# First layer of six experts by fifteen block products, with more buffers and later loads

## The chip, the core and the metric

The kernel runs on one NeuronCore of a Trainium2 chip. Its engines are TensorE (PE; its weight loads are listed apart, as PEld), VectorE (DVE), ScalarE (ACT), GpSimd (POOL) and SyncE (SP), each with a queue of its own that it works off in order, and 16 DMA engines that all queues share. The metric is the device time of one execution in microseconds, as the median of several runs; lower is better. All data is float32 unless marked.

## What is computed

1250 nodes with 768 features and 40,000 directed edges (and self-loops) go through a transformer-like block. Cut to what matters here:

```python
xn = layernorm(x)
x = x + gnn(xn, edges) + linear_attention(xn)        # two graph-attention layers; 12 heads
x = x + ffn(layernorm(x))

def ffn(xt):                                          # 1250 x 768, 8 experts, hidden 384
    gate = xt @ Wg + bg                               # 1250 x 8
    scores, idx = top_k(gate, 2)
    h = gelu(einsum('td,edh->eth', xt, W1) + b1)      # first layer, W1[e] is 768 x 384
    y = einsum('eth,ehd->etd', h, W2) + b2            # second layer, W2[e] is 384 x 768
    comb = sum(one_hot(idx, 8) * scores)              # the two raw gate scores of a token
    return einsum('te,etd->td', comb, y)
```

The change concerns the first layer of the experts, which the kernel computes only for the tokens that chose the expert.

## The kernel before, in words

Up to about 865 us the kernel builds the graph's adjacency matrix, runs the two attention layers (lines 380 to 640), the linear attention (640 to 1040) and the router. The last stage of that, by pairs of 125-token tiles, writes the normalised tokens with their eight gate values to `xl_d` in DRAM (`finish`, L929; stores at L937 and L951) and the sum so far to `out`, and counts each token into a table of slots: `idx` gives, for every expert and every block of 128 places, the rows of `xl_d` that stand there. Already there, products of big matrices are done by seven products of quarters with sums beside them (`query`, and `P` in the loop over pairs).

The experts then run in a Python loop, unrolled, of eight slots. Every expert has `FIX` = 3 fixed blocks of 128 rows; what is over goes into extra blocks, of which the first is placed into the slots of experts 6 and 7 (`more_...`) and others into a loop at the end. One slot, for e = 0 to 6, consists of

- `inner` (L1081): the first layer. The result `hT` is hidden-major: three tiles of 128 hidden units by 384 tokens. For each hidden tile six matmuls (128 of the 768 features each) accumulate in a PSUM bank, W1's 128x128 block as the stationary operand and `xT` with 384 token columns as the moving one; ScalarE then applies Gelu with the bias from PSUM into SBUF (L1092). Expert 0 does its first block alone, and then the other two, since their rows come later.
- `gather` (L1060) of the next expert: three indirect DMAs on POOL's queue (L1065) fetch 128 rows each into `xg` (three buffers); TensorE transposes them into PSUM tiles `px` (L1074, six transposes of 128 a block, two banks), VectorE copies them to `xsT` (L1075), and a tiny copy takes the expert's gate column into `gates` (L1078).
- `give` (L1095) three times, once per block: ScalarE multiplies the output bias with the gate (`gb`, L1099), TensorE multiplies `hT`'s block with W2 in two halves of 384 columns (`py`, L1106, four banks), VectorE combines them as `ys = py * gate + gb` (L1108, two buffers of `ys`), and an indirect DMA on POOL's queue adds the 128 rows to `out` in DRAM (L1110). These scatter-adds touch the same tensor, so each waits until the one before has landed.
- two loads on SP's queue: the output bias of expert e+2 (L1175) and the weights of expert e+4 (`expert`, L745; W1 at L748, W2 at L750, 1152 KB each) into one of four weight buffers `w`, when that buffer's last reader is done.

The weights of experts 1 to 3 are requested behind the router's last instructions, as soon as their buffers come free. The framework draws up the order of each engine's queue from the program's order and from when it expects operands and buffers to be free, and sets all waits; the queues of a trace are therefore not quite in the program's order.

A float32 matmul is seen in the trace as two passes: an `x36` of the first layer is 18 matmuls.

## Time and profile before

| what | value |
|---|---|
| median of 3 runs | 1096.91 us (1096.15 to 1099.57) |
| the profiled execution | 1097.82 us, its span 1096.1 us, mean granted clock 0.986 |
| start of the expert stage (first row gather issued) | 865.48 us |
| first row gather landed, first transpose | 871.95 us |
| first layer of expert 1, 2, 3 begins on TensorE | 901.11, 926.34, 951.56 us |
| last matmul ends | 1085.87 us |
| TensorE, weight loads, VectorE, ScalarE, POOL busy | 1031.0, 701.6, 705.8, 359.9, 78.8 us |
| one pass of the first layer, 384 columns, by its own row | 486 ns (passes overlap) |
| L1108, L1075 on VectorE, one | 616, 552 ns |
| scatter-add from issue to landing, min / median / max | 5.4 / 5.7 / 9.0 us |
| row gather from issue to landing, min / median / max | 3.7 / 5.4 / 6.4 us |

How to read the profile: a group's row gives line, engine, operation, out<-in with shapes, count, then busy time, mean duration of one, and the idle time of the engine just before them with what ended it. Durations of matmuls overlap each other, so the rate of a stream is read from its start and end, or from the chain. The chain is the sequence of work that ended last, followed back from the end of the run; each line gives start, length and what it was. A line can be written "PE ph L1090 x36": engine, tile written, line, instructions. The last part of the run, from 865 us on, is the expert stage and all that this document is about.

### The profile page before, as it was taken

To read this page: it belongs to the slowest core of one execution; us is meant where nothing else is said; L and a number is where in the kernel's file an instruction comes from. 1 tells how busy PE (TensorE), PEld (TensorE's weight loads), DVE (VectorE), ACT (ScalarE), POOL (GpSimd) and SP (SyncE) were. 2 spreads that over 40 slices of the span, in tenths; PEclk is the share of its full clock that TensorE was granted. 3 is DMA by queue.
4 is the path that set the end of the run, shared out by engine and by line. 5 is a ranking of instruction groups with operands and counts; after the bars stand their busy time and mean duration, and the time that the engine had idled before them with its cause. 6 is when DMAs were issued, how large, how long until landed. Compare 5 with 4: busy or idle time off the path is not lost.

```text
span 1096.1 us, 12392 instructions
## 1 busy us (share of the span) xinstructions
PE 1031.0 (94%) x4630; PEld 701.6 (64%) x4630; DVE 705.8 (64%) x1460; ACT 359.9 (33%) x548; POOL 78.8 (7%) x106
## 2 busy tenths in 40 slices
PE   6999999999999999988999999999999499999996
PEld 5876666587878879544555555656665376666674
DVE  7866684697897957769687958686855522222321
ACT  4612226372728373283833121112110111111121
POOL 2000000000000000000001000000000122223321
PEclk9999999999999999999999999999999699999998
DMA  5060000000000002000035002021144847777534
GB/s 161 29 211 19 29 15 1 1 1 1 1 1 1 1 1 87 1 0 1 15 142 153 1 15 71 20 65 43 58 153 132 274 116 221 213 213 203 116 58 59
DMA packets 35412, 79.51 MB, mean 73 GB/s; under 512 B 7078, under 2 KB 15416, under 8 KB 35348
## 3 DMA queue, kind: packets, MB, share of 16 engines
q1 hardware_dynamic: 29588, 58.90, 16.8%
q0 software_dynamic: 5760, 19.78, 8.5%
q8 instruction: 37, 0.61, 0.2%
q14 instruction: 27, 0.22, 0.1%
HBM read 60.33 MB, written 18.34 MB: 72 GB/s over the span
## 4 chain that ended last, share of the span: by engine, by line
PE 73%; DVE 20%; DMA 2%; ACT 1%; issue 1%; POOL 0%; DVEq 0%; POOLq 0%; ACTq 0%
PE s L863 19%; PE mm L648 9%; PE ph L1090 9%; PE py L1106 8%; PE mm L477 8%; DVE scr L569 6%; DVE w L589 5%; DVE w L590 5%; PE ag L602 3%; PE mm L924 2%; PE ag L624 2%; PE ec L398 2%; PE mm L452 2%; PE px L1074 2%; PE rb L558 1%; PE mm L662 1%
## 5 line engine op out<-in xcount | busy, mean ns | idle before, releaser
L602 PE MATMUL ag<-kept,w 125*125 125x198 f32 x800 | 137.5, 333 | 5.1 <-DVE w L590 4.8
L602 PEld LDWEIGHTS ag<-kept,w 125*125 125x125 f32 x800 | 133.5, 188 | 9.0 <-DVE w L590 9.0
L1106 PE MATMUL py<-w,hT 128*128 128x384 f32 x300 | 100.9, 486 | 0.0
L1090 PE MATMUL ph<-xsT,w 128*128 128x384 f32 (+2 forms) x432 | 99.9, 390 | 0.0
L589 DVE TENSOR_TENSOR w<-v,w 125x1250 f32<-125x1250 f32 x60 | 86.3, 1453 | 6.0 <-ACT w L587 5.4
L648 PE MATMUL mm<-Wv_sb,xnT 128*125 128x384 f32 x240 | 85.6, 489 | 4.8 <-DVE kvacc L668 4.8
L1090 PEld LDWEIGHTS ph<-xsT,w 128*128 128x128 f32 x432 | 68.9, 191 | 30.3
L569 DVE CUSTOM_DVE_ANT_0 scr<-ss_row,mask 125x1250 bf16<-125x1250 f32 x60 | 87.2, 1453 | 1.6 <-ACT ss_row L560 1.2
L477 PE MATMUL mm<-Wg,xnT 128*125 128x400 f32 x240 | 87.7, 505 | 0.2 <-ACT xnT L367 0.2
L590 DVE SCALAR_TENSOR_TENSOR w<-w,AT 125x1250 f32<-125x1250 f32 x60 | 86.4, 1454 | 0.4
L588 ACT ACTIVATE v<-dn_row,sl 125x1250 f32<-125x1250 f32 x60 | 79.3, 1333 | 17.4 <-DVE w L589 16.9
L648 PE MATMUL mm<-Wk_sb,xnT 128*125 128x384 f32 x240 | 85.0, 487 | 0.0
L1108 DVE SCALAR_TENSOR_TENSOR ys<-py,gates,gb 128x384 f32<-128x384 f32 x50 | 30.3, 616 | 79.3 <-PE py L1106 54.7
L1106 PEld LDWEIGHTS py<-w,hT 128*128 128x128 f32 x300 | 55.1, 190 | 33.1
L1075 DVE COPY xsT<-px 128x384 f32<-128x384 f32 x50 | 25.8, 552 | 73.3 <-PE px L1074 73.3
L648 PEld LDWEIGHTS mm<-Wv_sb,xnT 128*125 128x125 f32 x240 | 42.5, 187 | 31.4 <-DVE kvacc L668 6.9
L477 PEld LDWEIGHTS mm<-Wg,xnT 128*125 128x125 f32 x240 | 42.5, 188 | 26.5 <-ACT xnT L367 0.9
L1099 ACT ACTIVATE gb<-spare,gates 128x768 f32<-128x768 f32 x24 | 22.4, 935 | 112.4 <-DVE ys L1108 94.8
L587 ACT ACTIVATE w<-up_row,s 125x1250 f32<-125x1250 f32 x40 | 53.2, 1331 | 17.7 <-PE ag L602 17.6
L648 PEld LDWEIGHTS mm<-Wk_sb,xnT 128*125 128x125 f32 x240 | 42.0, 187 | 22.7 <-issue 1.8
L863 PE MATMUL s<-w,xnT 128*125 128x384 f32 x150 | 55.4, 489 | 0.0
L863 PE MATMUL s<-w 128*125 128x384 f32 x150 | 53.9, 491 | 0.0
(328 smaller groups left out, 1515.1 us busy)
## 6 DMA issues: line engine op xcount, KB each, us to landing
w<-in_L_ffn_W_dram SPq DMA_DIRECT2D x18, 1152.0 KB
xt<-in_x_dram SPq DMA_DIRECT2D x20, 336.0 KB
out_dram<-xt SPq DMA_DIRECT2D x10, 336.0 KB
xl_d<-xl SPq DMA_DIRECT2D x10, 336.0 KB
spare<-in_L_ffn_b_dram SPq DMA_DIRECT2D x8, 384.0 KB
W_sb<-in_L_gnn_W_dram SPq DMA_DIRECT2D x1, 2304.0 KB
Wk_sb<-in_L_mix_Wk_dram SPq DMA_DIRECT2D x1, 2304.0 KB
Wv_sb<-in_L_mix_Wv_dram SPq DMA_DIRECT2D x1, 2304.0 KB
```

The source lines that it names most:

```text
L477: nc.tensor.matmul(ps[:PT, :2 * (CG + 2)], xnT[:, c, t * PT:(t + 1) * PT], Wg1[:, c, 2 * k:2 * k + 2].rearrange("p h c -> p (h c)"), start ...
L569: nc.vector.tensor_tensor_reduce(scr, ss_row, mask[:, t], 1.0, 0.0, ALU.mult, ALU.max, top[:, t:t + 1])
L587: nc.scalar.activation(w, up_row, AF.Exp, bias=ss[:, st:st + 1])
L588: nc.scalar.activation(v, dn_row, AF.Exp, bias=sl[:, st:st + 1])
L589: nc.vector.tensor_tensor(w, v, w, op=ALU.max)
L590: nc.vector.scalar_tensor_tensor(w, w, 2.0, AT[:, st, :N], op0=ALU.min, op1=ALU.mult)
L602: nc.tensor.matmul(ag[:, t // 2, o:o + CG], w[:, t * PT:(t + 1) * PT], gw[:, st, hd], start=st == 0 and t % 2 == 0, stop=st == NT - 1, ski ...
L648: nc.tensor.matmul(ps[:PT, :384], xnT[:, c, t * PT:(t + 1) * PT], w[:, c, half], start=c == 0, stop=c == KC - 1)
L863: nc.tensor.matmul(ps, left[:, c], right[:, c], start=start and c == 0, stop=c == n - 1, skip_group_check=True)
L1090: nc.tensor.matmul(ph[:, n], w[0][:, o:o + 128], xT[:, c, n], start=c == 0, stop=c == KC - 1)
L1106: nc.tensor.matmul(py[:, :384], hT[:, f, j * 128:(j + 1) * 128], w[:, o:o + 384], start=f == 0, stop=f == FC - 1)
L1108: nc.vector.scalar_tensor_tensor(ys[:, half], py[:, :384], gates, gb[:, half], op0=ALU.mult, op1=ALU.add)
```

## The change

The first layer of experts 1 to 6 is no longer 54 products of 128x128 blocks, run as 18 matmuls of 384 columns, but 45, run as 45 matmuls of 128 columns. W1 of an expert is seen as 3 (hidden) by 2 (halves of the features) blocks, the tokens as 2 by 3, each block being three tiles of 128x128 deep. Fifteen products of sums of such blocks replace the eighteen of the plain scheme: `WAYS[0]` gives the eleven sums or differences of weight blocks, `WAYS[1]` the eleven of token blocks, `PRODUCTS` the fifteen products, each with the bank that it opens or is accumulated onto, and the result blocks to which its bank is copied (by ScalarE) or added (by VectorE). The nine result blocks are gathered in `hT` in SBUF; the Gelu is then applied there, in place.

The weight sums of expert e+1 are handed to VectorE one by one between the products of expert e, and the token sums of expert e+1 stand behind its gather. The sums lie in memory that earlier stages left free (`xnT` and `kept`). For expert 1 both kinds stand in expert 0's slot, the weight sums between its `give`s. Expert 0, expert 7 and the extra blocks keep `inner`.

With it come other edits: all PSUM tiles of the stage come from one pool of eight banks; `xg` gets five buffers in place of three, `ys` three in place of two; the copies from `px` to `xsT` move from VectorE to ScalarE, except for expert 0; and the weights of experts 1, 2 and 3 are now loaded behind a tiny VectorE copy that writes a gate value of expert 1's first, second and third block into the weight buffer, so that each load starts only once these rows are there.

```diff
--- before.py
+++ after.py
@@ -64,6 +64,32 @@
     for s in ap.shape:
         n *= s
     return bass.AP(tensor=ap.tensor, offset=ap.offset, ap=[[0, parts], [1, n]])
+
+
+WAYS = ((("12", 5, 1, 6), ("13", 3, 1, 4), ("9", 1, -1, "13"), ("14", 3, -1, 1), ("15", 2, -1, "12"),
+         ("7", 1, 1, "15"), ("3", 2, -1, 6), ("8", 4, 1, 5), ("-2", 2, 1, "9"), ("1", 5, -1, 3),
+         ("5", 6, -1, 4)),
+        (("4", 5, -1, 2), ("2", 4, 1, 6), ("9", "2", -1, 3), ("14", 1, -1, "9"), ("7", 1, 1, 2),
+         ("11", 6, -1, 3), ("15", "7", -1, 5), ("3", "15", -1, 4), ("8", 3, -1, 5), ("1", 3, -1, 2),
+         ("5", 6, -1, 5)))
+
+
+PRODUCTS = (
+    ("6", None, 1, 1, (1, "="), (2, "=-")),
+    ("10", None, 2, 4, (1, "+"), (3, "=-"), (7, "=")),
+    ("12", None, "12", 5, (8, "="), (9, "=")),
+    ("4", None, 5, "4", (8, "-"), (5, "=-")),
+    ("9", None, "9", "9", (4, "=-"), (3, "-")),
+    ("14", "6", "14", "14", (4, "+")),
+    ("13", None, "13", 3, (3, "+"), (6, "=")),
+    ("7", "12", "7", "7", (2, "+")),
+    ("11", None, 4, "11", (4, "-"), (6, "+"), (9, "+")),
+    ("3", "4", "3", "3", (7, "+")),
+    ("8", None, "8", "8", (5, "-")),
+    ("2", None, "-2", "2", (3, "+")),
+    ("15", None, "15", "15", (2, "-"), (7, "-")),
+    ("1", "13", "1", "1", (5, "+")),
+    ("5", "8", "5", "5", (9, "+")))
 
 
 @with_exitstack
@@ -742,9 +768,13 @@
 
     fp = ctx.enter_context(tc.tile_pool(name="fp", bufs=1, side="right"))
 
-    def expert(w1, w2, b2, b):
+    def expert(w1, w2, b2, b, behind=None):
+
 
         t = wt.tile([128, KC, D], F32, name="w", bufs=4).rearrange("p c f -> p (c f)")
+        if behind is not None:
+            nc.vector.tensor_copy(t.rearrange("p (a f) -> p a f", a=2)[:1, :, 0],
+                                  behind.to_broadcast([1, 2]))
         nc.sync.dma_start(t[:, :KC * FF].rearrange("p (c f) -> p c f", c=KC),
                           w1.rearrange("(c p) f -> p c f", p=128))
         nc.sync.dma_start(t[:, KC * FF:].rearrange("p (c d) -> p c d", c=FC),
@@ -1047,33 +1077,87 @@
         free = rp.tile([128, NV], F32)
         nc.vector.tensor_scalar(free, inv, 0.0, nobody, op0=ALU.is_equal, op1=ALU.mult)
         nc.vector.scalar_tensor_tensor(idx[:, :NV], inv, -1.0, free, op0=ALU.add, op1=ALU.add)
-        for e in range(1, 4):
-            ring.append(expert(fW1[e], fW2[e], fb2[e] if e < 2 else None, spare[e % 2]))
 
 
     mix.close()
     sp = ctx.enter_context(tc.tile_pool(name="sp", bufs=2))
-    x_p = ctx.enter_context(tc.tile_pool(name="x_p", bufs=2, space=PSUM))
-    h_p = ctx.enter_context(tc.tile_pool(name="h_p", bufs=2, space=PSUM))
-    y_p = ctx.enter_context(tc.tile_pool(name="y_p", bufs=4, space=PSUM))
-
-    def gather(rows, e):
+    e_p = ctx.enter_context(tc.tile_pool(name="e_p", bufs=8, space=PSUM))
+    q3 = KC // 2
+    places = [xnT.rearrange("p c n -> p (c n)"), kept]
+    slot3 = lambda k: places[k % 2][:, k // 2 * q3 * 128:(k // 2 + 1) * q3 * 128].rearrange(
+        "p (c n) -> p c n", c=q3)
+
+    def bank():
+        return e_p.tile([128, 512], F32, name="ps")
+
+    def sums(blocks, side, at):
+
+        got = {k + 1: b for k, b in enumerate(blocks)}
+        todo = []
+        for k, (name, a, sign, b) in enumerate(WAYS[side]):
+            got[name] = slot3(at + k)
+
+            def make(name=name, a=a, sign=sign, b=b):
+                op = nc.vector.tensor_add if sign > 0 else nc.vector.tensor_sub
+                op(got[name], got[a], got[b])
+            todo.append(make)
+        return got, todo
+
+    def weight_sums(w, e):
+        v = w[0][:, :KC * FF].rearrange("p (g c f) -> p g c f", g=2, c=q3)
+        return sums([v[:, g, :, i * 128:(i + 1) * 128] for i in range(3) for g in range(2)], 0,
+                    e % 2 * len(WAYS[0]))
+
+    def token_sums(xT):
+        return sums([xT[:, g * q3:(g + 1) * q3, j * 128:(j + 1) * 128] for g in range(2)
+                     for j in range(3)], 1, 2 * len(WAYS[0]))
+
+    def inner15(A, B, bias, between):
+
+
+        hT = sp.tile([128, FC, FIX * 128], F32, name="hT")
+        C = [hT[:, i, j * 128:(j + 1) * 128] for i in range(3) for j in range(3)]
+        banks = {}
+        for name, onto, a, b, *uses in PRODUCTS:
+            ps = banks[name] = banks[onto] if onto else bank()
+            for c in range(q3):
+                nc.tensor.matmul(ps[:, :128], A[a][:, c], B[b][:, c], start=c == 0 and not onto,
+                                 stop=c == q3 - 1, skip_group_check=True)
+            for to, how in uses:
+                to = C[to - 1]
+                if how == "=":
+                    nc.scalar.copy(to, ps[:, :128])
+                elif how == "=-":
+                    nc.scalar.mul(to, ps[:, :128], -1.0)
+                elif how == "+":
+                    nc.vector.tensor_add(to, to, ps[:, :128])
+                else:
+                    nc.vector.tensor_sub(to, to, ps[:, :128])
+            if between:
+                between.pop(0)()
+        while between:
+            between.pop(0)()
+        for f in range(FC):
+            nc.scalar.activation(hT[:, f], hT[:, f], AF.Gelu, bias=bias[:, f])
+        return hT
+
+    def gather(rows, e, copy=nc.vector.tensor_copy):
 
         got = []
         for r in rows:
-            xg = sp.tile([128, D + NE], F32, name="xg", bufs=3)
+            xg = sp.tile([128, D + NE], F32, name="xg", bufs=5)
             nc.gpsimd.indirect_dma_start(xg, None, xl_d, bass.IndirectOffsetOnAxis(r, 0))
             got.append(xg)
         xT = sp.tile([128, KC, FIX * 128], F32, name="xsT")
         gates = sp.tile([128, FIX], F32, name="gates")
         for j, xg in enumerate(got):
             for a in range(2):
-                px = x_p.tile([128, 512], F32, name="px")
+                px = bank()
                 for c in range(3):
                     o = (3 * a + c) * 128
                     nc.tensor.transpose(px[:, c * 128:(c + 1) * 128], xg[:, o:o + 128], ident)
-                nc.vector.tensor_copy(xT[:, 3 * a:3 * a + 3, j * 128:(j + 1) * 128],
-                                      px[:, :384].rearrange("p (b n) -> p b n", b=3))
+                copy(xT[:, 3 * a:3 * a + 3, j * 128:(j + 1) * 128],
+                     px[:, :384].rearrange("p (b n) -> p b n", b=3))
             at = slice(D + e, D + e + 1) if isinstance(e, int) else bass.ds(e + D, 1)
             nc.vector.tensor_copy(gates[:, j:j + 1], xg[:, at])
         return xT, gates
@@ -1084,7 +1168,7 @@
             hT = sp.tile([128, FC, FIX * 128], F32, name="hT")
         n = slice(a * 128, b * 128)
         for f in range(FC):
-            ph = h_p.tile([128, 512], F32, name="ph")
+            ph = bank()
             for c in range(KC):
                 o = c * FF + f * 128
                 nc.tensor.matmul(ph[:, n], w[0][:, o:o + 128], xT[:, c, n], start=c == 0,
@@ -1097,10 +1181,10 @@
         w, wb = w
         gb = sp.tile([128, D], F32, name="gb")
         nc.scalar.mul(gb, wb, gates)
-        ys = sp.tile([128, D], F32, name="ys")
+        ys = sp.tile([128, D], F32, name="ys", bufs=3)
         for k in range(2):
             half = slice(k * 384, (k + 1) * 384)
-            py = y_p.tile([128, 512], F32, name="py")
+            py = bank()
             for f in range(FC):
                 o = KC * FF + f * D + k * 384
                 nc.tensor.matmul(py[:, :384], hT[:, f, j * 128:(j + 1) * 128], w[:, o:o + 384],
@@ -1153,24 +1237,41 @@
         nc.vector.tensor_mul(pick, vals, mine)
         one = fp.tile([128, 1], F32, name="one", bufs=2)
         nc.vector.tensor_reduce(one, pick, AX.X, ALU.add)
-        pr = h_p.tile([128, 512], F32, name="ph")
+        pr = bank()
         nc.tensor.transpose(pr[:1, :128], one, ident)
         nc.vector.tensor_scalar(row, pr[:1, :128], add, None, op0=ALU.add)
 
     for e in range(NE - 1):
         xT, gates = ahead
         bias = fb1T[:, :, e:e + 1]
+        between = []
+        if 0 < e < NE - 2:
+            A, between = weight_sums(ring[e + 1], e + 1)
         if e:
-            hT = inner(ring[e], xT, bias)
+            hT = inner15(now, B, bias, between)
+            now = A
         else:
             hT = inner(ring[e], xT, bias, 0, 1)
             inner(ring[e], xT, bias, 1, FIX, hT)
-        ahead = gather(fixed(e + 1), e + 1)
+        ahead = gather(fixed(e + 1), e + 1, nc.scalar.copy)
+        if e == 0:
+            for n in range(1, 4):
+                ring.append(expert(fW1[n], fW2[n], fb2[n] if n < 2 else None, spare[n % 2],
+                                   ahead[1][:1, n - 1:n]))
+        todo = []
+        if e < NE - 2:
+            B, todo = token_sums(ahead[0])
+        if e == 0:
+            now, between = weight_sums(ring[1], 1)
+        for make in todo:
+            make()
         if e == NE - 2:
             ee, more_rows, more_bias, more_w = first
             more_xT, more_gates = gather([more_rows], ee)
         for j, rows in enumerate(fixed(e)):
             give(ring[e], hT, j, rows, gates[:, j:j + 1])
+            for make in between[j * 6:(j + 1) * 6]:
+                make()
         if e + 2 < NE:
             nc.sync.dma_start(spare[e % 2], row_bcast(fb2[e + 2], 128))
         if e + 4 < NE:
```

## The prediction

> **What bounds the kernel now.** I read the page first (busy shares, the chain), then the chain in order of time through the experts, then a table of stretches, then groups and queues of that part.
>
> ```profile
> PE 1031.0 (94%) x4630; PEld 701.6 (64%) x4630; DVE 705.8 (64%) x1460; ACT 359.9 (33%) x548; POOL 78.8 (7%) x106
> PE 73%; DVE 20%; DMA 2%; ACT 1%; issue 1%; POOL 0%; DVEq 0%; POOLq 0%; ACTq 0%
> ```
>
> TensorE is busy almost throughout. The chain from the router's end on:
>
> ```profile
> 865.48 6.42 DMA xg<-xl_d,idx
> ...
> 901.27 11.61 PE ph L1090 x36
> 916.18 10.32 PE py L1106 x32
> 926.50 11.61 PE ph L1090 x36
> 941.40 10.32 PE py L1106 x32
> ...
> 1039.94 3.71 DMA xg<-xl_d,rows
> ...
> 1054.31 8.04 PE ph L1090 x72
> ```
>
> Experts follow every 25.2 us (901.27, 926.50) and the chain never leaves TensorE. A logical f32 product is two passes: 36 passes of 384 columns take 11.61 us, 322.5 ns each, and the 72 passes of 128 columns late in the run take 8.04 us, 111.7 ns each. Two row gathers are on the chain as transfers: the first (6.42 us) and the one for the extra block (3.71 us).
>
> ```profile
> 864.00:868.00 4.00, 0.58 (x2) 0.11 (x2) 0.93 (x7) 0.00 (x0) 2.03 (x2) 0.50 1.04 406
> 868.00:872.00 4.00, 0.05 (x1) 0.06 (x1) 0.07 (x1) 0.00 (x0) 0.95 (x1) 0.50 0.90 353
> 926.30:951.60 25.30, 25.30 (x92) 15.50 (x91) 6.91 (x15) 4.54 (x6) 7.70 (x6) 1.00 0.76 203
> ```
>
> The columns are the stretch, its length, busy time of PE, PEld, DVE, ACT, POOL, then granted clock, DMA share and GB/s. During the first gather the DMA engines are full and TensorE is idle; in an expert's stretch TensorE has no gap, while VectorE works 6.91 of 25.30 us and ScalarE 4.54.
>
> ```profile
> 919.70 1.61 POOL L1110 DMA_INDIRECT out_dram<-ys,idx  x1 [2.13 <-DVE ys L1108]
> 927.68 1.59 POOL L1110 DMA_INDIRECT out_dram<-ys,idx  x1 [6.37 <-DVE ys L1108]
> 937.36 1.55 POOL L1110 DMA_INDIRECT out_dram<-ys,idx  x1 [8.09 <-DMA out_dram<-ys,idx]
> 944.92 1.61 POOL L1110 DMA_INDIRECT out_dram<-ys,idx  x1 [2.14 <-DVE ys L1108]
> ```
>
> The scatter-adds run one at a time: 7.98, 9.68 and 7.56 us from start to start, a second chain almost as long as an expert.
>
> **The change, part by part.**
>
> *The products.* For experts 1 to 6, 36 passes of 384 columns (11.61 us) become 15 products of 3 matmuls, 90 passes of 128 columns. At 111.7 ns that is 10.05 us: 1.56 us saved per expert, 9.4 us over six. The row is the same operand shape, each pass with its own weight load, so I take it. Neighbours bound it: the 36 passes from 1066.05 last 4.18 us with their tail, 116 ns (10.45 us, 7.0 saved); a third of the wide pass, 107.5 ns, would give 9.68 us (11.6 saved). Transposes (2.0 us) and the second layer (36 passes, 11.6 us) stay, so the expert's floor is 23.7 us.
>
> *What VectorE gets.* Per expert 22 sums of 384 elements and 16 additions of 128 from PSUM; it loses six copies (L1075, 552 ns).
>
> ```profile
> L1018 DVE TENSOR_TENSOR xt<-xt,s 125x384 f32<-125x384 f32 x25 | 13.7, 552 | 36.5 <-PE s L863 36.4
> L960 DVE TENSOR_TENSOR eq<-eq,before 125x64 f32<-125x64 f32 x10 | 2.2, 224 | 0.2
> L1092 ACT ACTIVATE hT<-ph,fb1T 128x384 f32<-128x384 f32 x18 | 10.4, 580 | 46.7 <-PE ph L1090 46.7
> L726 ACT COPY kept<-mm 128x128 f32<-128x128 f32 x6 | 1.6, 272 | 2.6 <-PE mm L725 2.6
> ```
>
> A sum is 0.55 us; between 224 ns for 64 elements and 552 for 384, an addition of 128 is about 0.29. Busy time: 6.9 - 3.3 + 22 x 0.55 + 16 x 0.29 = 20.3 of 23.7 us. It fits, but the place matters. During the products VectorE has 11 weight sums of the next expert, the 16 additions and two leftover L1108 (1.2 us). Back to back the pair at 846.73 (2 in 1.02 us) gives 0.46 per sum, and 0.21 per addition by the same overlap: 5.1 + 3.4 + 1.2 = 9.7 us. Each waiting for the end of the one before: 11 x 0.58 + 16 x 0.31 + 1.2 = 12.6 us. Available are the products' 10.05 us and 2.0 us of the next expert's transposes, less 0.9 us for the last Gelu (0.58) and its handoffs: 11.15. Loss per expert: 0 to 1.45 us. The sums seldom use the one just before, the additions wait for a product each, so I mix: 5.1 + 5.0 + 1.2 = 11.3, a loss of about 0.2, 1.2 us over six. The 11 token sums (5.1 us) lie beside the second layer (11.6 us, with 3.7 us of L1108).
>
> *ScalarE* gets nine copies (0.27 us) and the six copies from VectorE (0.48 each): 4.5 + 2.5 + 2.9 = 9.9 of 23.7 us, hidden; were they not, each copy delays an addition, priced below.
>
> *Eight shared banks.* Ten new banks per expert in order, all read out long before their reuse; only the last of the fifteen ("5") goes back soon, to the bank of "8", the eleventh, some 2 us after that one's reader may start. That is inside the 0.2.
>
> *Third buffer of L1108.* VectorE waits 24.5 us in seven waits for scatter-adds; 3.9 us of it stand at the start of each expert's products. That was free on an idle VectorE; with additions queued behind, it would cost. With three buffers the slot needs the landing of the scatter-add of one expert earlier, which has some 7 us of slack. Taken as nothing; without it, see the scatter rival.
>
> *Loads of experts 1 to 3.* They leave the stretch 840 to 862 and wait for three tiny VectorE copies (0.15 us each) after expert 1's rows, so on SP's queue the bias row of expert 1 waits too. SP has no other issue before 895. The gain is at the router's end: VectorE's wait of 0.90 us at 857.92 for a store goes (bounds 0 to 0.9; I take 0.9, since nothing else fills the DMA engines), and the first gather lands in 3.71 us, as the late one with free engines does, in place of 6.42 (bounds 0 and 2.7; I take 2.7). Together 3.6. What is late next: the loads start near 873 and bring 7.1 MB; at 380 GB/s of 864 to 872 they are done by 892, expert 1's first layer by 879. Its weight sums (5.1 us) are wanted at about 897. Were the rate the mean 213 GB/s of 840 to 960, expert 2's first layer would land at 892, wanted at 897: still nothing.
>
> *Five row buffers.* POOL can fetch the extra block's rows ahead; TensorE's 0.83 us wait at 1043.78 goes. On POOL's queue the gathers only move earlier. In expert 0's slot VectorE has 22 sums and 3.7 us, 13.8 us against 11.6, but idles from 877 on: 0, at worst 2 us once.
>
> *Sum.* -9.4 - 3.6 - 0.8 + 1.2 = -12.6 us. The profiled execution took 1097.8 us (0.9 above the median of 1096.9); 1097.8 - 12.6 = **1085.3 us** (1097.82 unrounded).
>
> **The rivals.**
>
> *Late Gelu (13%).* The order puts the transposes ahead of the last products, so nothing covers the last addition and Gelu: 1.1 us per expert in place of 0.2. For: before, transposes and second-layer products alternate. Against: they alternate for want of banks (two), and come after the first layer. 1097.8 - 13.8 + 6.6 = 1090.6.
>
> *Scatter-adds bind (8%).* A slot needs between 23.9 (third one at the undisturbed 6.2 us) and 25.2 us, the expert 23.7. Only five slots have weight loads beside them and the third buffer holds one scatter-add, so a lag of 5 x 0.9 us should fit. If it does not: 1085.3 + 4.7 = 1090.0.
>
> *The start does not move (7%).* The first gather is late for another reason than the loads: 1085.3 + 3.6 = 1088.9.
>
> *Slower: VectorE's handoffs (16%).* In its in-order queue every addition stands behind ScalarE's first copy of that block, and each such wait holds the sums behind it. L655, which waits for ScalarE, idles 5.8 us over 20, 0.29 each. With nine such waits on the 12.6 us VectorE needs 15.2 us, 4.05 over the 11.15: 1097.8 - 13.8 + 6 x 4.05 = 1108.3. It decides from 13.45 us on, a loss of 2.3 per expert. Against: ScalarE is little used, and copies come a product or more ahead.
>
> *Slower: narrow passes pay for their weights (3%).* If each pass costs the load's own 190 ns (mean of L1090's loads), 90 take 17.1 us: 1085.3 + 9.4 + 6 x 5.5 = 1127.7; even with the old time overall at 137 ns. Against: 72 such passes with their loads took 8.04 us, the clock granted at 1.00.
> [...]
>
> **How the numbers follow.** The forecast has 53%, with a range of its own of 1081 to 1089 (products at 107.5 or 116 ns, start 0 to 3.6, VectorE 0 to 1.45). The rest: 13, 8, 7, 16 and 3. About 0.3%, 3.3 us, is what a measurement tells from no change, so "same" is 1093.6 to 1100.2; 3 of the late Gelu's 13 and 3 of the handoffs' 16 fall there. Faster: 53 + 10 + 8 + 7 = 78%; same 6%; slower 13 + 3 = 16%. The range 1081 to 1097 takes in all but the slower cases and the forecast's edge, about 80%.
>
> **What would show it.** Right: experts every 23.7 to 23.9 us, 90 passes of L1090's successor in about 10.1 us without gaps, VectorE near 20 busy us per expert, first gather landing in under 4.5 us, no wait at the extra block. Wrong: TensorE idle before a product (banks, VectorE) or before the second layer (ScalarE's Gelu); L1108 waiting for a scatter-add; passes above 120 ns; expert 1 waiting for its load.

## The result, and the profile after

The changed kernel took 1085.53 us (median of five runs, 1084.88 to 1091.11), the kernel before 1097.86 us (five runs, 1096.15 to 1103.96). The ratio is 0.9887, with a 95% interval of 0.9858 to 0.9916: 1.1% faster. The prediction was 1085.3 us, faster, with a range of 1081 to 1097. The sum came out almost to the microsecond, but not every term of it did, and two extra buffers that the prediction had priced at nothing (`ys`) and at 0.8 us (`xg`) turned out to be worth 13.4 and 9.6 us inside the changed kernel.

The profiled execution is the slowest of the five, 1091.11 us with a span of 1089.4. It is 5.6 us late already in code that the change does not touch: the eighteen matmuls of the router's last pair start at 834.17 us, against 828.61 before. The comparisons below therefore count from these eighteen matmuls, the anchor. From there to the end of the span it is 267.5 us before and 255.2 after, 12.3 us less, which is about the difference of the medians too.

The page's busy shares, and its sum of the chain by engine, after:

```profile
PE 1027.8 (94%) x4954; PEld 728.6 (67%) x4954; DVE 767.6 (70%) x1649; ACT 386.8 (36%) x644; POOL 92.1 (8%) x106
PE 74%; DVE 20%; DMA 1%; ACT 1%; issue 1%; POOL 0%; DVEq 0%; POOLq 0%; ACTq 0%
```

TensorE has 324 passes more (6 x 54) and is nevertheless busy 3.2 us less; VectorE gains 61.8 us of work and in this profile the chain still never goes through it in the experts. The chain in order of time, after (start, length, engine, tile, line, count; L1124 the block products, L1158 the transposes, L1190 the second layer, L1174 the old first layer of experts 0 and 7):

```profile
834.17 5.88 PE s L893 x18
...
870.58 4.57 DMA xg<-xl_d,idx
875.19 2.82 PE ps L1158 x12
...
878.44 12.41 PE ps L1174 x72
...
904.43 10.05 PE ps L1124 x90
914.48 1.97 PE ps L1158 x18
916.45 11.61 PE ps L1190 x36
928.06 10.05 PE ps L1124 x90
...
1022.84 10.05 PE ps L1124 x90
1032.89 2.62 PE ps L1158 x24
1035.51 11.61 PE ps L1190 x36
1047.12 8.04 PE ps L1174 x72
```

Ninety narrow passes take 10.05 us where 36 wide ones took 11.61. Expert follows expert after 23.63 us (904.43 to 928.06), with 18 transposes between the products and the second layer. The transfer at 870.58 is that of expert 0's second block; the first block's rows, issued at 869.22, are there for the first transpose at 873.47, and the table below counts from these. The transfer of the extra block's rows is gone from the chain, and its six transposes follow the others without a wait (24 in 2.62 us).

The table of stretches, after, for one whole slot each (stretch, length, busy time of PE, PEld, DVE, ACT, POOL, granted clock, DMA share, GB/s):

```profile
904.30:927.90 23.60, 23.60 (x146) 18.83 (x145) 18.97 (x51) 8.63 (x21) 8.25 (x6) 1.00 0.72 189
927.90:951.50 23.60, 23.60 (x145) 18.85 (x144) 17.20 (x48) 8.51 (x21) 8.80 (x6) 1.00 0.79 217
```

In these two slots TensorE has no gap. VectorE, 6.91 us before, now works 17 to 19 of 23.6 us. By parts, from the anchor (each the difference of two starts in the two profiles, in us):

| part | before | after | difference |
|---|---|---|---|
| anchor to first row gather issued | 36.87 | 35.05 | -1.8 |
| issue to first transpose | 6.47 | 4.25 | -2.2 |
| first transpose to expert 1's first layer | 29.32 | 30.96 | +1.6 |
| expert 1's first layer to expert 7's | 153.04 | 142.69 | -10.35 |
| expert 7's first layer to the end | 41.79 | 42.28 | +0.5 |
| sum | 267.49 | 255.23 | -12.3 |

The third line is a loss that the prediction did not have; most of it is the clock, told under the hardware at the end.

### The profile page after: what moved, and what is told of

Read it like the earlier page. It is cut to its first block, busy times and chain, and to the rows that moved or that the text cites. A ratio compares the mean times of both kernels' runs of the same rounds, so it can differ in the third digit from the quotient of the medians.

```text
span 1089.4 us, 13352 instructions
## 1 busy us (share of the span) xinstructions
PE 1027.8 (94%) x4954; PEld 728.6 (67%) x4954; DVE 767.6 (70%) x1649; ACT 386.8 (36%) x644; POOL 92.1 (8%) x106
## 4 chain that ended last, share of the span: by engine, by line
PE 74%; DVE 20%; DMA 1%; ACT 1%; issue 1%; POOL 0%; DVEq 0%; POOLq 0%; ACTq 0%
PE s L893 19%; PE mm L674 9%; PE ps L1190 8%; PE mm L503 8%; DVE scr L595 6%; PE ps L1124 6%; DVE w L615 5%; DVE w L616 5%; PE ag L628 3%; PE mm L954 2%; PE ag L650 2%; PE ps L1174 2%; PE mm L478 2%; PE ec L424 2%; PE ps L1158 2%; PE g L972 1%
## 5 line engine op out<-in xcount | busy, mean ns | idle before, releaser
L1190 PE MATMUL ps<-w,hT 128*128 128x384 f32 x300 | 98.4, 486 | 0.0
L1190 PEld LDWEIGHTS ps<-w,hT 128*128 128x128 f32 x300 | 56.2, 190 | 37.1
L1192 DVE SCALAR_TENSOR_TENSOR ys<-ps,gates,gb 128x384 f32<-128x384 f32 x50 | 29.4, 612 | 51.5 <-PE ps L1190 36.6
L503 PEld LDWEIGHTS mm<-Wg,xnT 128*125 128x125 f32 x240 | 42.7, 189 | 26.4 <-ACT xnT L393 0.8
L1149 POOL DMA_INDIRECT xg<-xl_d,idx x24 | 30.7, 1280 | 298.3 <-DVE one L1239 278.9
L1194 POOL DMA_INDIRECT out_dram<-ys,idx x24 | 43.8, 1826 | 111.3 <-DMA out_dram<-ys,idx 20.9
L431 DVE TENSOR_TENSOR AT<-AT,ec 125x120 f32 x162 | 44.5, 275 | 11.6 <-PE ec L424 8.7
L650 PE MATMUL ag<-w,h 125*97 125x417 f32 (+1 forms) x120 | 46.7, 532 | 4.8 <-DVE w L616 4.8
```

The source lines that it names most:

```text
L503: nc.tensor.matmul(ps[:PT, :2 * (CG + 2)], xnT[:, c, t * PT:(t + 1) * PT], Wg1[:, c, 2 * k:2 * k + 2].rearrange("p h c -> p (h c)"), start ...
L650: nc.tensor.matmul(ag[:, i, :b - a], h2[:, st, hd * (C2 + 1):(hd + 1) * (C2 + 1)], w[:, a:b], start=st == 0, stop=st == NT - 1)
L1190: nc.tensor.matmul(py[:, :384], hT[:, f, j * 128:(j + 1) * 128], w[:, o:o + 384], start=f == 0, stop=f == FC - 1)
```

## The experiments

Each experiment is one edit of the changed kernel, but for `loads_alone`, which edits the kernel before, `after_again`, which has no edit, and the last, which has three. Times are medians; the ratio stands to the kernel before on the same chip. A difference from the changed kernel is one between two medians, most of them from different chips; the intervals of the ratios, 0.15 to 0.3% to each side, mean that it is good to some 2 to 3 us.

### wide: the products undone

Everything else of the change is kept, and the first layer of experts 1 to 6 is again 18 matmuls of 384 columns, without any sums.

```diff
-            hT = inner15(now, B, bias, between)
-            now = A
+            hT = inner(ring[e], xT, bias)
...
-        if e < NE - 2:
-            B, todo = token_sums(ahead[0])
-        if e == 0:
-            now, between = weight_sums(ring[1], 1)
```

> The changed kernel with experts 1 to 6 on the plain first layer again (36 passes of 384 columns, no sums, no additions); banks, buffers, the copies on ScalarE and the late loads stay. Theory (the gain is TensorE's pass count): the distance from one expert's first layer to the next goes from 23.6 back to 25.2 us, 9.4 to 9.7 us in all, so about 1095 us. Rival (most of the gain comes from buffers and loads): 1088 us or less.

Measured: 1093.24 us (1092.66 to 1099.67), ratio 0.996 [0.9933, 0.9988]. From the chain:

```profile
897.76 11.61 PE ps L1174 x36
...
922.94 11.61 PE ps L1174 x36
```

An expert takes 25.18 us again (897.76 to 922.94), and from expert 1's first layer to expert 7's it is 151.78 us, 9.1 more than with the products. Add the 0.27 us that the changed kernel loses in its fourth and fifth slot (23.75 and 23.78 us, from the chain, for 23.63), and the products are worth the predicted 9.4 us by themselves, counted in these two profiles.

### loads_alone: the late loads without the rest

The kernel before, with only the loads of experts 1 to 3 moved behind the copies of expert 1's gates.

```diff
-        for e in range(1, 4):
-            ring.append(expert(fW1[e], fW2[e], fb2[e] if e < 2 else None, spare[e % 2]))
...
         ahead = gather(fixed(e + 1), e + 1)
+        if e == 0:
+            for n in range(1, 4):
+                ring.append(expert(fW1[n], fW2[n], fb2[n] if n < 2 else None, spare[n % 2],
+                                   ahead[1][:1, n - 1:n]))
```

> The kernel before with one part of the change alone: the loads of experts 1 to 3 wait for expert 1's rows (no sums, three row buffers, plain first layer). Theory (late loads free the DMA engines at the router's end): the first gather is issued 1.8 us earlier and lands 2.2 us sooner, 1094 to 1095 us. Rival (the 7 us that early loads cost the changed kernel came only from weight sums that slipped into VectorE's queue ahead of the router's last steps, and there are no sums here): 1097 to 1098.5 us, no change.

Measured: 1094.94 us (1093.09 to 1098.82) against 1098.62, ratio 0.9965 [0.9951, 0.9978]: 3.7 us (by the interval 2.4 to 5.4), where 3.6 were predicted. The chain:

```profile
868.59 3.97 DMA xg<-xl_d,idx
872.60 1.54 PE px L1075 x6
...
902.01 11.61 PE ph L1091 x36
...
1040.67 3.79 DMA xg<-xl_d,rows
```

The first gather lands in 3.97 us (6.42 before), 2.5 us gained, and it is issued 1.8 us earlier (35.07 us after the anchor for 36.87). Slots keep 25.22 us, and the extra block's gather is still on the chain: the five row buffers, not the loads, took it away.

### early_loads: all but the late loads

```diff
+        for n in range(1, 4):
+            ring.append(expert(fW1[n], fW2[n], fb2[n] if n < 2 else None, spare[n % 2]))
...
-        if e == 0:
-            for n in range(1, 4):
-                ring.append(expert(fW1[n], fW2[n], fb2[n] if n < 2 else None, spare[n % 2],
-                                   ahead[1][:1, n - 1:n]))
```

> The changed kernel with the loads of experts 1 to 3 at their old place, without the wait on expert 1's rows. Theory (the late loads gain at the start): the first row gather takes 6.4 us to land in place of 4.3 and the router's end loses up to 1.8 us, so 2 to 4 us longer, 1087.5 to 1089.5 us. Rival (the late loads only push transfers into expert 0's slot, where a gather for expert 2 took 7.4 us on POOL and the first scatter-add left late): the scatter-adds start earlier and the time is 1083 to 1086 us.

Measured: 1092.36 us (1091.52 to 1094.13), ratio 0.9941 [0.9916, 0.9966]: 6.8 us worse than the changed kernel, twice what the theory gave. The slots are 23.62 us as before; all of it is lost before the first gather, which is issued 42.09 us after the anchor (828.06 to 870.15) rather than 35.05. VectorE's instructions in order of time, between the router's last steps (start, length, line, out<-in):

```profile
862.55 0.55 DVE L1104 TENSOR_TENSOR xnT<-w,xnT 128x384 f32<-128x384 f32 x1
863.02 0.22 DVE L990 TENSOR_TENSOR eq<-eq,before 125x64 f32<-125x64 f32 x1
863.16 0.55 DVE L1104 TENSOR_TENSOR kept<-w,xnT 128x384 f32<-128x384 f32 x1
863.62 0.22 DVE L991 TENSOR_TENSOR gt<-gt,eq 125x64 f32<-125x64 f32 x1
863.76 0.55 DVE L1104 TENSOR_TENSOR xnT<-w 128x384 f32<-128x384 f32 x1
```

L1104 are the weight sums. With the weights there early, the framework puts 22 of them (experts 1 and 2, 0.47 us each back to back) into VectorE's queue between the router's last steps; the first of them makes VectorE stand 2.51 us for a weight load (at 845.39), and from 860 to 868 VectorE has no idle time (8.00 of 8.00 us). The gather itself is then as quick as in the changed kernel, 4.10 us from issue to first transpose. So in the changed kernel the late loads hold back work, not only traffic: the tiny copy that delays the load also delays the sums that read it. Without the sums the late loads are worth 3.7 us, with them 6.8.

### two_ys: two buffers for what a slot gives

```diff
-        ys = sp.tile([128, D], F32, name="ys", bufs=3)
+        ys = sp.tile([128, D], F32, name="ys", bufs=2)
```

> The changed kernel with two buffers for what a slot gives in place of three. Theory (VectorE would stand at a scatter-add with additions queued behind it): TensorE waits at each expert, 1 to 3 us per expert for five experts, 1090 to 1100 us. Rival (the wait is covered as before, so the third buffer is worth nothing): 1085 to 1087 us.

Measured: 1098.93 us (1096.61 to 1102.45), ratio 1.0016 [1.0, 1.0032]. The third buffer carries 13.4 us, as much as the whole change gains; the edits guard one another, so that what the experiments give for each does not add up to the change. The waits of this run over the experts (engine, line, what it waited for: us in total, times, longest), and one of the stops in order of time:

```profile
DVE ys L1192 <- DMA out_dram<-ys,idx: 36.0, 6, 7.1
...
PE ps L1124 <- ACT hT L1129: 9.2, 6, 2.5
```

```profile
929.18 1.14 DVE L1192 SCALAR_TENSOR_TENSOR ys<-ps,gates,gb 128x384 f32<-128x384 f32 x2 [6.38 <-DMA out_dram<-ys,idx]
...
930.42 0.94 ACT L1183 ACTIVATE gb<-spare,gates 128x768 f32<-128x768 f32 x1 [3.26 <-DVE ys L1192]
...
931.26 0.26 ACT L1131 ACTIVATE hT<-ps 128x128 f32<-128x128 f32 x1
931.42 0.59 ACT L1129 COPY hT<-ps 128x128 f32<-128x128 f32 x3
...
932.06 0.94 PE L1124 MATMUL ps<-xnT,kept 128*128 128x128 f32 x6 [1.36 <-ACT hT L1129]
```

VectorE stands 6.38 us for a scatter-add. The next `gb` on ScalarE waits for VectorE, and behind `gb`, in ScalarE's queue, stand the copies that empty the product banks; so TensorE finds no bank for its next product. It is a chain through three in-order queues, and the slots become 25.1 to 26.4 us. From expert 1's to expert 7's first layer this run takes 153.2 us, as much as the kernel before.

### three_xg: three row buffers

```diff
-            xg = sp.tile([128, D + NE], F32, name="xg", bufs=5)
+            xg = sp.tile([128, D + NE], F32, name="xg", bufs=3)
```

> The changed kernel with three row buffers in place of five. Theory (five buffers only fetch the extra block's rows ahead): TensorE's 0.8 us wait there comes back, 1086 to 1087 us. Rival (expert 1's rows, and with them the three weight loads and expert 1's weight sums, come so late that its products wait): 1088 to 1092 us.

Measured: 1095.17 us (1092.6 to 1100.31), ratio 0.9976 [0.9958, 0.9993], 9.6 us worse than the changed kernel. Only the last slot changes. From the chain:

```profile
1022.57 5.43 DMA out_dram<-ys,idx
...
1028.76 1.55 POOL out_dram L1194
...
1030.62 5.22 DMA xg<-xl_d,rows
...
1035.98 1.51 PE ps L1158 x6
1037.49 13.92 PE ps L1190 x36
1051.41 8.04 PE ps L1174 x72
```

The extra block's gather needs a buffer that comes free only in the slot; by then two scatter-adds stand ahead of it on POOL's queue, each waiting for the one before. It is issued at 1030.62, and TensorE waits 6.43 us. After that wait the clock has dropped, and the second layer takes 13.92 us for 11.61:

```profile
1030.00:1036.00 6.00, 0.02 (x1) 0.05 (x1) 0.00 (x0) 0.82 (x3) 1.33 (x2) 0.65 0.69 132
1036.00:1040.00 4.00, 4.00 (x11) 2.79 (x12) 1.11 (x2) 0.00 (x0) 0.00 (x0) 0.50 0.02 4
1040.00:1044.00 4.00, 4.00 (x11) 2.29 (x10) 0.91 (x2) 0.00 (x0) 0.00 (x0) 0.75 0.00 0
```

With five buffers it had been issued 2.8 us before expert 6's products began (1020.05, the products at 1022.84); here it is 13.1 us after (1030.62 and 1017.53). The 6.43 us of wait, 0.9 of transposes and 2.3 of second layer at the lower clock make 9.6.

### sums_twice: twice the weight sums

Each weight sum is computed twice in succession, 11 x 0.47 = 5.1 us more for VectorE per expert. The result is the same.

```diff
                 op(got[name], got[a], got[b])
+                if side == 0:
+                    op(got[name], got[a], got[b])
```

> The changed kernel with every weight sum computed twice (11 more sums of 384 elements per expert, 5.1 us more on VectorE, beside the products of experts 1 to 5). Theory of the prediction (VectorE needs 11.3 us beside the products and has 11.15): every microsecond more shows, 5 x 5.3 = 26 us, about 1112 us. Rival (VectorE has some 5 us of room per expert, because weight sums may slide past the products): 1086 to 1092 us.

Measured: 1095.51 us (1092.83 to 1099.31), ratio 0.9969 [0.9951, 0.9987], 10.0 us more than the changed kernel: between what the two theories gave. The slots are 29.42, 23.62, 25.45, 24.04, 28.41 and 24.28 us. TensorE stands and then runs slowly:

```profile
902.99 0.94 PE L1126 MATMUL ps<-xnT 128*128 128x128 f32 x6 [2.02 <-ACT hT L1131]
...
904.59 1.48 PE L1126 MATMUL ps<-kept 128*128 128x128 f32 x6
```

VectorE is full from 896 to 912 (16.00 of 16.00 us), the additions are late, ScalarE's copies behind them too, and a bank is not free. The wait of 2.02 us is followed by a granted clock of 0.57 over 904 to 908. In the same slot the framework put the transposes ahead of the last product, so that the second layer then stood for the Gelu:

```profile
913.81 11.88 PE L1192 MATMUL ps<-w,hT 128*128 128x384 f32 x36 [1.48 <-ACT hT L1143]
```

That is what the rival "late Gelu" of the prediction describes, here once. The prediction's way of pricing this, all work beside the products against 11.15 us available, gives 11.3 + 5.1 - 11.15 = 5.2 us for each of five experts and is too strict, since three slots (the first, third and fifth) pay nearly all of it; why these and not the others stays open. What is shown is that VectorE has no room for 5.1 us more at this place in its queue.

### vector_copies: the row copies back on VectorE

```diff
-        ahead = gather(fixed(e + 1), e + 1, nc.scalar.copy)
+        ahead = gather(fixed(e + 1), e + 1)
```

> The changed kernel with the copies of the transposed rows on VectorE again for all experts (six of 0.55 us each). Theory (VectorE has about 3 us of room per expert, as doubling 5.1 us of sums cost 2.0 us): 0 to 0.5 us per expert, 1085.5 to 1088.5 us. Rival (the copies stand in VectorE's queue behind leftover weight sums and hold up the banks and the token sums): 1090 us or more.

Measured: 1091.66 us (1087.66 to 1097.99), ratio 0.9944 [0.9922, 0.9966], 6.3 us worse. Six copies of 548 ns, 3.3 us per expert, are put on VectorE, and slots become 24.3 to 25.1 us. TensorE's only waits in the experts are again for a bank that ScalarE has not emptied:

```profile
PE ps L1124 <- ACT hT L1129: 3.6, 5, 1.2
```

That is 3.6 us in five waits. So 3.3 us more at this place in VectorE's queue already cost time, although VectorE works only 17 to 19 of 23.6 us in the changed kernel. Whether the amount binds or, as the rival has it, the order of the queue is not told apart.

### fewer_adds: a scatter-add less per expert

The scatter-add of the middle block of experts 0 to 5 is left out.

```diff
-        nc.gpsimd.indirect_dma_start(out, bass.IndirectOffsetOnAxis(rows, 0), ys, None,
-                                     compute_op=ALU.add)
+        if add:
+            nc.gpsimd.indirect_dma_start(out, bass.IndirectOffsetOnAxis(rows, 0), ys, None,
+                                         compute_op=ALU.add)
...
-            give(ring[e], hT, j, rows, gates[:, j:j + 1])
+            give(ring[e], hT, j, rows, gates[:, j:j + 1], j != 1 or e > 5)
```

> The changed kernel, leaving out the scatter-add of the middle block of experts 0 to 5 (their rows lack that part; all matmuls stay). Theory (TensorE sets the pace, and the scatter-adds only touch the very end, where the last one starts 1.1 us after its rows are ready): 1084 to 1085.5 us. Rival (the chain of scatter-adds holds up the experts): 1082 us or less.

Measured: 1084.6 us (1082.83 to 1085.55), ratio 0.9868 [0.9853, 0.9883]; the 0.9 us that it is below the changed kernel are within the noise. The slots are 23.62 us each, the last 24.28, and from expert 7's first layer to the end it is 41.85 us (42.28 in the changed kernel). So with three buffers the chain of scatter-adds costs at most 0.3 us within the experts and 0.4 at the end, in these two profiles.

### first_block: multiply expert 0's first block before turning the others

The changed kernel transposes all three blocks of expert 0 before its first matmul, and the profiled run lost 1.6 us in that slot. The theory was that transposes at the start hold the granted clock down.

```diff
-        for j, xg in enumerate(got):
+        def turn_block(j, xg):
...
             hT = inner(ring[e], xT, bias, 0, 1)
+            for turn_next in rest:
+                turn_next()
             inner(ring[e], xT, bias, 1, FIX, hT)
```

> The changed kernel with expert 0's first block multiplied before the rows of its other two blocks are transposed. Theory (in the changed order TensorE runs 18 transposes first, and its granted clock stays at half for them, so that expert 0's slot takes 31.0 us against 29.3 before): the slot loses 1 to 1.6 us, about 1084 us. Rival (the clock rises a fixed time after TensorE starts, whatever it runs): within 0.5 us of the changed kernel, 1085 to 1086 us.

Measured: 1086.68 us (1083.45 to 1087.5), ratio 0.9881 [0.9864, 0.9898], no gain. The theory falls, by this run and the next.

### after_again: the changed kernel once more

The same kernel, with another profile.

> The changed kernel itself, beside the three below on one chip, so that a microsecond can be told. All theories: 1085 to 1087 us.

Measured: 1085.33 us (1083.49 to 1086.08), ratio 0.9879 [0.9858, 0.99]. From its chain, expert 0's slot:

```profile
868.37 2.28 PE ps L1158 x12
...
870.87 11.79 PE ps L1174 x72
```

The same instructions in the same order, and 72 passes take 11.79 us where the other profile has 12.41, 12 transposes 2.28 for 2.82. From first transpose (866.54) to expert 1 (896.24) it is 29.70 us here, 30.96 in the other profile and 29.32 before: of the 1.6 us in the third line of the table, 1.3 is not the change's doing, and 0.4 remains. The clock (columns as above, the number behind the five engines) rises here while TensorE runs transposes, and nothing else since it began at 866.54:

```profile
869.54:870.54 1.00, 1.00 (x9) 0.97 (x8) 0.98 (x4) 1.00 (x1) 0.48 (x2) 0.80 0.94 304
```

In this profile TensorE waits once, 0.73 us, in expert 1's products for ScalarE's copy, and that slot takes 24.62 us (896.24 to 920.86), 0.99 over 23.63.

### extras_late: the search for extra blocks behind expert 1

The first gather is issued when VectorE has done some small steps that only the extra blocks need (L1218 to L1239 in the changed kernel). They were moved, in the program, into expert 1's slot.

```diff
-    more = fp.tile([128, NE, NJ - FIX], F32)
...
+        if e == 1:
+            more = fp.tile([128, NE, NJ - FIX], F32)
...
```

> The changed kernel with the steps that find the extra blocks (from L1216 to L1242: small VectorE instructions and two transposes) moved behind expert 1's slot. Theory (some nine of them stand in VectorE's queue ahead of the row numbers, and the first gather waits for them): the first gather is issued 1 to 2 us earlier after the router's last products, 1083.5 to 1084.5 us. Rival (the first gather waits for the landing of the last tokens' store): issued at the same distance, within 0.5 us of the changed kernel.

Measured: 1085.47 us (1084.96 to 1090.43), ratio 0.9897 [0.9872, 0.9921], no change. But the edit did not do what it says. The chain:

```profile
862.64 0.14 DVE idx L1079
...
863.40 0.21 DVE one L1271 x2
...
863.83 1.06 POOL xg L1149
```

The framework still puts these steps into VectorE's queue between the last steps that the gather needs. `idx`, its list of rows, is done at 862.78, and the gather is issued at 863.83. What releases it, the last small step or the landing of the last store to `xl_d`, is not told apart and stays open. In ten of the other thirteen profiles (`two_ys`, `sums_twice` and `first_block` left aside) the gather leaves some 1.05 us after `idx`, in `early_loads` too, where the last rows for that store were done 8.3 us before the gather (861.89) and not 5.8 as in the changed kernel, `wide`, `extras_late`, `vector_copies` and `better`; that speaks against the store, but does not settle it.

### better: three edits together

`first_block`, `extras_late` and the token sums dealt out behind the three `give`s.

```diff
-        for make in todo:
-            make()
...
-            for make in between[j * 6:(j + 1) * 6]:
+            for make in todo[j * 4:(j + 1) * 4] + between[j * 6:(j + 1) * 6]:
                 make()
```

> The changed kernel with expert 0's first block multiplied ahead of the other transposes, the search for extra blocks behind expert 1's slot, and the token sums dealt out behind the three second-layer blocks. Theory: 1 us from expert 0's slot, 1 to 2 us from an earlier first gather, nothing elsewhere, 1082 to 1083.5 us. Rival (the token sums come too late, and the next products wait): 1086 us or more.

Measured: 1087.54 us (1083.98 to 1091.69), ratio 0.9902 [0.9876, 0.9929], not better than the changed kernel, which no variant beat by more than the noise. The slots are 23.63 us, the sum of TensorE's own work, but for the first with 24.01 and the last with the extra block, so there was next to nothing left to gain from VectorE's order.

## Why the prediction was right, point by point

*The products: right.* The price came from the 72 passes of 128 columns late in the trace of before, 111.7 ns each; 90 in 10.05 us are 111.7 ns. `wide` gives the term by itself, 9.1 of 9.4 us. Each narrow pass with its own weight load pays little for it: 111.7 ns, where a third of a wide pass is 107.5. The loads (192 ns by their row, busy 18.8 of 23.6 us) lie beside other passes. The runs show 111.7 and 322.5 ns for 128 and 384 columns, within 4% of proportion, and the rival of narrow passes that pay for their weights, which was to show above 120 ns, is out.

*VectorE: right in direction, too dear.* Predicted 20.3 busy us per expert and a loss of 0.2; measured 17.2 to 19.0 us and no loss in four of the six slots. It also charged the loss to six slots, though no weight sums stand beside expert 6's products. The sums overlap (0.47 us apart rather than 0.55), which the prediction used for the products' part but not for the busy time. Two slots hold 0.12 and 0.15 us over 23.63 (the sixth's 0.65 are the extra block's transposes), and `after_again` loses 0.99 us in one slot: 0.3 and 1.0 us where 1.2 were predicted. The rival of slower handoffs did not come true, but `sums_twice` and `vector_copies` show that it was near: 3.3 us more at that place in VectorE's queue cost time, and its in-order queue does feed back to TensorE, mostly through the banks and once, in `sums_twice`, through the Gelu (1.48 us).

*ScalarE hidden: right.* 8.5 to 8.6 busy us against 9.9, and the late Gelu did not come in the changed kernel: in the chain the 18 transposes stand between the products and the second layer in every slot, and TensorE has no wait there.

*The start: right in the sum, wrong in the parts.* 3.6 predicted, 3.7 alone, 4.0 in the changed kernel: the earlier issue is worth 1.8 (predicted 0.9) and the landing 2.2 (predicted 2.7). Why the landing is 4.25 rather than 3.71 is not shown; the number of gathers that leave together does not explain it, since with three row buffers it is 4.01 (`loads_alone`) and 4.14 (`three_xg`). The step that failed is the reason given for the earlier issue, one wait of VectorE for a store of 0.90 us. That wait is gone, but the gather also left 2.0 us after its list of rows `idx` was done in the kernel before (863.47 to 865.48), and 1.05 in `loads_alone` (867.54 to 868.59); these other 0.9 us the prediction did not see, and what held the gather there stays open. And the late loads also keep the sums out of the router's end, 3 us that the prediction did not see, since it took the sums' place from the program.

*Five row buffers: right on the path, incomplete as a price.* The wait at the extra block is gone, 0.83 us, and 0.2 with it for transposes that ran slower behind it (0.85 for 0.65 us). But the value of the edit in the changed kernel is 9.6 us: with scatter-adds lagging, a gather behind them on POOL's queue makes TensorE wait 6.43 us (`three_xg`). "On POOL's queue the gathers only move earlier" is true and is the point; the prediction priced it against the old queue.

*Third buffer: "taken as nothing" was its effect on the sum, not its worth.* Its absence was referred to the rival of scatter-adds, 1090; `two_ys` measures 1098.9. The rival had the slot bound by POOL's chain (4.7 us); the real loss runs through `gb` on ScalarE to the product banks. The slack of some 7 us that the prediction gave the third buffer was not there either: with three buffers scatter-adds still make VectorE wait:

```profile
DVE ys L1192 <- DMA out_dram<-ys,idx: 14.9, 5, 3.1
```

That is 14.9 us in five waits over the experts, the longest 3.1, and it is hidden. That scatter-adds do not bind is shown by `fewer_adds`.

*The sum.* Against the forecast -12.6 stand -12.3 measured from the anchor. Experts 1 to 6 give -10.35, forecast -9.0 (-9.4, -0.8 and +1.2): six slots of 25.23 against 23.63 us, 9.6, of which the products are 9.4, with 1.03 at the extra block and 0.27 lost. The start gives -4.0 (-3.6), the end +0.5 (0), and expert 0's slot +1.6 (0), of which 1.3 is the late clock. In `after_again`, whose clock rises early, anchor to end is 254.5 us (827.27 to 1081.8), 13.0 less than before. So part of the closeness is luck: a VectorE term too dear and a start too cheap stood against a clock and an end that the prediction had not reckoned with.

## What to carry to other kernels

Trading wide matmuls for fewer, narrower ones on TensorE pays as far as the time per column stays equal (here 111.7 ns for 128 columns and 322.5 for 384), which a stretch of the same shape in the old trace tells; then the work is to keep the other queues from handing their delay to TensorE, and buffers that look like small change (one more output tile, two more row tiles) can be worth as much as the arithmetic (13.4 and 9.6 us here, and 9.4). When an engine works off a queue in order, ask of each wait what stands behind it and on which engine the next one will stand, three engines far. And work made ready early is not free: a scheduler may put it ahead of the critical chain, as with the 22 sums of `early_loads`.

## What the runs showed of the hardware that was not expected

*The rise of the granted clock comes in two kinds.* At the start of the experts TensorE comes out of an idle stretch at a granted clock of 0.50. A stretch of a microsecond (columns as above; the number behind the five engines is the clock), of the kernel before, whose first transpose starts at 871.95:

```profile
875.00:876.00 1.00, 1.00 (x11) 0.93 (x9) 0.68 (x3) 0.78 (x1) 0.39 (x1) 0.96 0.72 130
```

and of the changed kernel, whose first transpose starts at 873.47:

```profile
878.00:879.00 1.00, 1.00 (x7) 0.97 (x5) 0.95 (x4) 0.00 (x0) 0.71 (x1) 0.50 0.81 310
879.00:880.00 1.00, 1.00 (x8) 1.00 (x8) 0.38 (x4) 0.00 (x0) 0.23 (x1) 0.69 0.95 298
```

About 3 us after the first transpose in one, about 6 in the other. Of the fourteen profiles eight rise after some 3 to 4 us and six (the changed kernel's first, `early_loads`, `two_ys`, `three_xg`, `fewer_adds`, `better`) after some 6 to 8. The two profiles of one and the same kernel fall in different groups, so it is not the order of the instructions. Between these two it is worth 1.3 us (30.96 and 29.70 us from first transpose to expert 1). What puts a profile into one group or the other is not shown.

*A wait can have a second price.* After 6.43 us of waiting in `three_xg` the clock stood at 0.50 (1036 to 1040) and 36 passes took 13.92 us for 11.61; in `sums_twice` a wait of 2.02 us was followed by 0.57 over 904 to 908. Not every wait of that length has it: after waits of 2.50 and 2.03 us in `two_ys` the passes kept their pace, six in 0.67 us (907.58 to 908.25, 958.75 to 959.42).

*POOL's DMA issues lengthen with VectorE's sums.* Before, a scatter-add took POOL 1.55 to 1.63 us; after, up to 3.29 (1.95 in `after_again`), and with the sums doubled, in `sums_twice`, up to 6.43. Behind the last of the sums (at 1016.10 in the changed kernel) all ten scatter-adds that are left, from 1023.41 on, take 1.55 to 1.61 us again, also the one at 1029.78, beside additions from PSUM. A short and a long one of the changed kernel, in order of time:

```profile
912.83 1.56 POOL L1194 DMA_INDIRECT out_dram<-ys,idx  x1 [7.62 <-DVE xnT L1102]
920.46 2.83 POOL L1194 DMA_INDIRECT out_dram<-ys,idx  x1 [6.07 <-DMA out_dram<-ys,idx]
```

The longer one lies beside token sums, VectorE instructions that follow each other without a gap from 919.91 to 921.78. But the short one lies beside VectorE work too, weight sums and additions from PSUM in turn; which of the sums do it is not shown. One row gather, at 891.78, took POOL 7.36 us; the DMA engines were busy throughout (share 1.05, 410 GB/s) and so was VectorE, with sums. Full DMA engines alone do not do it: in the kernel before, the gathers at 866.84 and 868.11 took 0.97 and 0.95 us (share 1.04 and 1.10, 421 and 452 GB/s), with VectorE idle. How the sums lengthen an issue is not shown.
